# Softplus sums and dt times x on GpSimd, and an autoregressive part read from four token phases, in a hybrid scan, attention and spectral-convolution kernel

## Chip, cores and metric

The kernel runs on one core of one Trainium2 chip. The metric is the device time of one execution in microseconds; the median of several executions is quoted. Before the change it took 7304.48 us (three runs, 7297.25 to 7325.35).

## The reference, cut to what matters

Four images of 48 x 48 tokens with 128 channels pass two layers. The first has a selective scan in four directions:

```python
dt = softplus(dts + dt_proj_b)                      # 256 channels, 2304 tokens, 4 directions
def step(h, inp):
    dA = exp(dt_l[..., None] * A)                   # 16 states per channel
    h = h * dA + (dt_l * u_l)[..., None] * B_l
    y = einsum('bkdn,bkn->bkd', h, C_l)
# ... norm, gate, projection; then attention over 2304 tokens; then
def _stu(u, ...):                                   # four sequence lengths T, T/2, T/4, T/8
    return _compute_spectral(...) + _compute_ar_u(Mu, u)    # 16 long convolutions; 3 taps: u(t), u(t-1), u(t-2)
```

The change touches softplus and `dt * u` in the scan, and `_compute_ar_u`.

## The kernel before

Names used below: rep is a half's dt and dt * x, repeated for the states; bc is a row of B or C, spread over the partitions; xd holds a chunk's projected x; M are the mixture's matrices, G the convolution's output weights made from them, tt its filter tiles; a burst is a row of transfers or of GpSimd operations issued together.

An image's scan is one stage of 24 chunks (4 directions x 6 chunks of 384 tokens). A chunk has 8 units j = 0 to 7: two halves h of the channels times four groups q of the states. Stage 0 runs beside the "mixture" that prepares the convolution's weights; stages 1 to 3 run beside the convolution of the image before; the last convolution runs alone. Here is the preparation of a chunk, a generator that the scan loop advances by one `yield` twice a unit:

```python
ps = mm_tile(f"dt{name}_{h}")                                  # for each half h
nc.tensor.matmul(ps[:, :CS], dtw[:, k, h * P:(h + 1) * P], xd[:R + 1], start=True, stop=True)
nc.scalar.activation(re[:, h, 1], ps[:, :CS], AF.Abs)
nc.scalar.activation(re[:, h, 0], ps[:, :CS], AF.Relu)
# ... both halves: e = exp(-|.|), u = e + 1, l = ln(u), u = u - 1; then for each half h:
ps = mm_tile(f"sp{name}_{h}")
for i, (w, t) in enumerate(((ident, e[:, h]), (nident, u[:, h]), (ident, l[:, h]), (ident, re[:, h, 0]))):
    nc.tensor.matmul(ps[:, :CS], w, t, start=(i == 0), stop=(i == 3))       # softplus as a sum in PSUM
nc.scalar.copy(re[:, h, 0], ps[:, :CS])
nc.vector.tensor_tensor(re[:, h, 1]..., ps[:, :CS]..., x, ALU.mult)         # dt * x
# ... store re to DRAM; one unit after the other:  load(0), then load(1):
rep = pool.rep.tile([P, 2, G4, CS], F32, tag="rep", ...)
for c in range(C4):
    nc.sync.dma_start(rep[c * DL:(c + 1) * DL], d[h])                       # 4 x 384 KB
```

A unit multiplies by B (GpSimd for three of the eight units, `POOLED`, VectorE for the others), scans four times on VectorE, and multiplies by C on GpSimd; TensorE then sums the states into y. An engine takes its instructions in the program's order, here that of the scan loop:

```python
POOLED = ((0, 3), (1, 1), (1, 3))
enter(s)                              # B product: GpSimd for a pooled unit s+2, VectorE for unit s+1
units[s].scan(0, ...)                 # exp on ScalarE into PSUM, scan on VectorE
units[s - 1].times_c()                # GpSimd, 128x1536
units[s].scan(1, ...)
prepare(s)                            # one step of the next chunk's preparation (two chunks' for j = 4 and 5)
more((s + 0.5) / len(units))          # mixture or convolution, in equal shares of TensorE columns
units[s].scan(2, ...); units[s].scan(3, ...)
units[s - 2].sum_c(...)               # y on TensorE, waits for times_c of s-2
more(...); prepare(s)
```

The mixture loads its matrices M right ahead of use, and the convolution's short loads G and tt come from the same queue, SP's, as the rep loads:

```python
for k in range(KF):                   # mixture
    M = [pool.two.tile([P, NF, C], F32, tag=f"M{j}", ...) for j in range(2)]
    for t, src in zip(M, ("M_phi_plus", "M_phi_minus")):
        nc.sync.dma_start(t, a[src][:, k].rearrange("i d e -> d i e"))
# autoregressive part: tap j reads tokens (4 m + phase - j), a step of 4 tokens
src = now["x"][:, 2 - j:2 - j + 4 * w].rearrange("p (m r f) -> p f r m", f=2, r=2)
nc.tensor.matmul(p[:, :, :, :v], now["mu"][:, x, j, :], src[:, :, :, :v], ...)
```

Of the kernel before, what the change touches and what calls it, by code (L numbers as in the profile page):

```python
# [15 lines left out]
P = 128  # L16
B, H, W, C = 4, 48, 48, 128
L = H * W
# [34 lines left out]
def hybrid_kernel(ctx: ExitStack, tc: tile.TileContext, a: dict, out: bass.AP):  # L53
# [75 lines left out]

    zs = res.tile([NH, P, L], F32, name="zd")  # L130
    td = res.tile([L, C], F32, name="td")
    ud = res.tile([P, 2 + L], F32, name="ud")
    gd = res.tile([KF, P, 2, 2 * NF - 2, C], F32, name="gd")
    mud = res.tile([P, 2 * NF - 2, 3, C], F32, name="mud")
    fd = res.tile([KF, 3, 2, LF + P], F32, name="fd")
# [150 lines left out]
    class Chunk:  # L286
# [16 lines left out]
        def prep(self, pool):  # L303




            k, name, xc = self.k, self.name, xcs[self.b]
            yield
            xd = self.xd = pool.xd.tile([64, CS], F32, tag="xd", name=f"xd{name}")  # L310
            bcd = self.bcd = dram.tile([32, CS], F32, tag="bcd", name=f"bcd{name}")
            ps = mm_tile(f"xp{name}")
            for h in range(NH):
                nc.tensor.matmul(ps[:64, :CS], xw[:, h, k, :], in_order(xc[h], k, self.lo, CS),  # L314
                                 start=(h == 0), stop=(h == NH - 1))
            yield 2 * CS
            nc.scalar.activation(xd, ps[:64, :CS], AF.Identity, bias=onerow)
            yield

            u, l = [pool.one.tile([P, NH, CS], F32, tag=f"tmp{v}", name=f"{v}{name}") for v in "ul"]  # L320
            re = pool.one.tile([P, NH, 2, CS], F32, tag="re", name=f"re{name}")
            for h in range(NH):
                ps = mm_tile(f"dt{name}_{h}")
                nc.tensor.matmul(ps[:, :CS], dtw[:, k, h * P:(h + 1) * P], xd[:R + 1], start=True, stop=True)  # L324
                yield CS
                nc.scalar.activation(re[:, h, 1], ps[:, :CS], AF.Abs)
                nc.scalar.activation(re[:, h, 0], ps[:, :CS], AF.Relu)
                if h == 0:
                    nc.sync.dma_start(bcd, xd[32:64])
                yield  # L330
            e = re[:, :, 1]
            yield 0
            nc.scalar.activation(e, e, AF.Exp, scale=-1.0)
            nc.scalar.activation(u, e, AF.Identity, bias=1.0)
            yield
            yield 0
            nc.scalar.activation(l, u, AF.Ln)
            nc.scalar.activation(u, u, AF.Identity, bias=mone)
            d = dram.tile([NH, DL, 2, G4, CS], F32, tag="dtdu", name=f"dtdud{name}")

            def store(h):
                for g in range(G4):
                    nc.sync.dma_start(d[h, :, :, g], re[g * DL:(g + 1) * DL, h])

            def load(h):
                rep = pool.rep.tile([P, 2, G4, CS], F32, tag="rep", name=f"rep{name}_{h}")
                for c in range(C4):
                    nc.sync.dma_start(rep[c * DL:(c + 1) * DL], d[h])
                self.rep.append(rep)

            yield
            for h in range(NH):
                ps = mm_tile(f"sp{name}_{h}")
                for i, (w, t) in enumerate(((ident, e[:, h]), (nident, u[:, h]), (ident, l[:, h]), (ident, re[:, h, 0]))):
                    nc.tensor.matmul(ps[:, :CS], w, t, start=(i == 0), stop=(i == 3))  # L355
                yield 4 * CS

                nc.scalar.copy(re[:, h, 0], ps[:, :CS])
                x = in_order(xc[h], k, self.lo, CS)
                w = x.shape[2]  # L360
                nc.vector.tensor_tensor(re[:, h, 1].rearrange("p (r w) -> p r w", w=w),  # L361
                                        ps[:, :CS].rearrange("p (r w) -> p r w", w=w), x, ALU.mult)
                if h == 1:
                    store(0)
                yield
            yield 0
            store(1)
            load(0)
            yield
            yield 0  # L370
            load(1)
            yield

        def fetch(self, i, pool):
# [62 lines left out]
    EARLY = 4  # L437
    FETCHED = sorted({q for h, q in POOLED} | set(range(Q4, 2 * Q4)))

    CHUNK_COLS = (len(quads) - len(POOLED)) * CS + len(quads) * CS + 12 * CS  # L440

    def begin_scans(b, pool):

# [12 lines left out]
    def scans(b, chunks, preps, front, back, work, work_cols):  # L456

        units = [Unit(ch, h, q) for ch in chunks for h, q in quads]
        total = len(chunks) * CHUNK_COLS + work_cols
        done = [0]  # L460

        def more(share):

            while done[0] < share * total:
                cols = next(work, None)
                if cols is None:
                    break
                done[0] += cols

        def enter(s):  # L470

            if s + 2 < len(units) and units[s + 2].pool:
                units[s + 2].enter(back.s)
            if 0 <= s + 1 < len(units) and not units[s + 1].pool:
                units[s + 1].enter(back.s)

        def spread(s):
            if s < len(units) and not units[s].pool:
                units[s].spread(back.psB)
                done[0] += CS  # L480

        def prepare(s):

            ci, j = divmod(s, len(quads))
            for c in [ci + 1] * (j <= TURN + 1) + [ci + 2] * (j >= TURN):
                if c < len(chunks):
                    done[0] += next(preps[c], None) or 0

        def refill(s, i):

            if 0 <= s < len(units) and s // len(quads) + 1 < len(chunks):
                u, nxt = units[s], chunks[s // len(quads) + 1]
                if u.h == NH - 1:
                    nxt.fetch(i + u.q, front)

        pending = []
        spread(0)
        enter(-2)
        enter(-1)
        spread(1)  # L500
        for s in range(len(units) + 2):
            real = s < len(units)
            if pending and real:
                pending.pop().add_y()
            enter(s)
            if real:
                units[s].scan(0, back.psa)
            if 1 <= s <= len(units):
                units[s - 1].times_c()
            if real:  # L510
                units[s].scan(1, back.psa)
            prepare(s)
            more((s + 0.5) / len(units))
            spread(s + 2)
            if real:
                units[s].scan(2, back.psa)
                units[s].scan(3, back.psa)
            if pending:
                pending.pop().add_y()
            refill(s - 3, Q4)  # L520
            if s + 1 < len(units) and units[s + 1].pool:
                refill(s + 1, 0)
            if s >= 2:
                units[s - 2].sum_c(back.psy)
                done[0] += CS
                if units[s - 2].q == Q4 - 1:
                    pending.append(units[s - 2])
            more((s + 1) / len(units))
            prepare(s)
        for u in pending:  # L530
            u.add_y()
        assert next(work, None) is None
# [225 lines left out]
    def begin_stu(b, T, pool, ps):  # L758
# [7 lines left out]
        whole = L // 512  # L766
        nc.sync.dma_start(t[:, :whole], td[:512 * whole].rearrange("(J p j) c -> p J j c", p=P, j=4))
        nc.sync.dma_start(t[:KP[-1], whole], td[512 * whole:].rearrange("(p j) c -> p j c", j=4))
        uT = pool.one.tile([P, 2 + L], F32, tag="uT", name=f"uT{b}")
        nc.vector.memset(uT[:, 0:2], 0.0)  # L770
        yield
        for J in range(NM):
            k = KP[J]
# [3 lines left out]
            p = ps.pss.tile([P, 512], F32, tag="s", name=f"utr{b}_{J}")  # L777
            for j in range(4):
                nc.tensor.transpose(p[:, j * k:(j + 1) * k], u[:k, J, j], ident[:k, :k])
            nc.scalar.copy(uT[:, 2 + 512 * J:2 + 512 * J + 4 * k].rearrange("c (p j) -> c j p", j=4),  # L780
                           p[:, :4 * k].rearrange("c (j p) -> c j p", j=4))
        nc.sync.dma_start(ud, uT)

    STU_COLS = sum(KF * 12 * sum(hi - max(lo, J * P) for J in range((hi + P - 1) // P))
# [2 lines left out]
    def stu(b, pool, ps):  # L787
# [86 lines left out]
        def begin(n):  # L874
            (lo, hi, place, extra), k = items[n]
            m = 2 if extra else 1
            now["x"] = pool.one.tile([P, 2 + 512], F32, tag="ux", name=f"ux{b}_{n}")
            nc.sync.dma_start(now["x"][:, :2 + 4 * (hi - lo)], ud[:, 4 * lo:4 * hi + 2])
            now["mu"] = pool.one.tile([P, 2, 3, C], F32, tag="mue", name=f"mue{b}_{n}")
            nc.sync.dma_start(now["mu"][:, :m], mud[:, place:place + m])  # L880
            now["T", n] = pool.two.tile([P, 4, C], F32, tag="res", name=f"res{b}_{n}")
# [6 lines left out]
        def ar(n):  # L888
# [4 lines left out]
            now["p"] = p = p[:, :4 * w].rearrange("p (f r m) -> p f r m", f=2, r=2)  # L893
            for i, (v, x) in enumerate(parts(w, extra)):
                for j in range(3):
                    src = now["x"][:, 2 - j:2 - j + 4 * w].rearrange("p (m r f) -> p f r m", f=2, r=2)
                    nc.tensor.matmul(p[:, :, :, :v], now["mu"][:, x, j, :], src[:, :, :, :v],  # L897
                                     start=(i == 0 and j == 0), stop=False)
            yield 3 * 4 * (w + extra)
# [70 lines left out]
    activate(0)  # L970
    turn.close()
    begin0.close()
    front = Stage(tc, "f0", "left", one=(1, SB), xd=(3, SB), rep=(3, SB))
    begun = last(begin_scans(0, front))
    start_y(0)
    once = Stage(tc, "once", "right", one=(1, SB))
# [2 lines left out]
    for b in range(B):  # L979
# [24 lines left out]
        turn.close()  # L1004
        if b + 1 < B:
            activate(b + 1)
            front = Stage(tc, f"f{b + 1}", "left", one=(1, SB), xd=(3, SB), rep=(3, SB))
            pieces = begin_scans(b + 1, front)
        else:
            pieces = iter(())  # L1010
# [67 lines left out]
```

## Time and profile before

Engine names: PE is TensorE's matmuls, DVE VectorE, ACT ScalarE, POOL GpSimd, SP the queue from which nearly all transfers are issued. A stage runs from its first scan to its last.

| stretch of the profiled run | us |
|---|---|
| stage 0 (with the mixture) | 1055.5 |
| stages 1, 2, 3 (with a convolution) | 1351.6, 1345.2, 1336.5 |
| last convolution | 1026 |
| between them (attention, norms, start) | 1183 |

Stages 1 to 3 in the view of busy time by window; the columns are window, length, busy time (and number) of PE, PEld, DVE, ACT, POOL, then granted TensorE clock, DMA share, GB/s:

```profile
1555.10:2906.70 1351.60, 1287.80 (x5760) 733.50 (x5760) 1076.34 (x1305) 618.19 (x1177) 930.32 (x423) 0.97 0.67 174
3249.30:4594.50 1345.20, 1280.45 (x5760) 728.70 (x5760) 1076.45 (x1305) 618.14 (x1177) 930.35 (x423) 0.98 0.67 174
4935.10:6271.60 1336.50, 1272.04 (x5764) 723.37 (x5766) 1075.94 (x1305) 618.26 (x1177) 930.23 (x423) 0.99 0.68 176
```

The page's slices of the granted clock, its chain of waits by engine, and the median landing time of a rep load (last figure) in its list of transfers:

```profile
PEclk6777777979999998979999999879999999889999
...
PE 67%; DVE 18%; DMA 6%; ACT 3%; POOL 2%; issue 2%; SPq 2%; DVEq 0%; POOLq 0%; ACTq 0%
...
rep<-dtdud SPq DMA_DIRECT2D x768, 384.0 KB, 7.9
```

And TensorE's own waits over the whole run (total us, times, longest):

```profile
PE y L424 <- POOL s L416: 153.1, 66, 5.6
...
PE G L750 <- DMA M<-in_M_phi_plus: 103.4, 16, 7.3
...
PE pr L907 <- DMA G<-gd: 38.0, 13, 7.3
PE cv L851 <- DMA tt<-fd: 33.6, 13, 8.4
```

### The profile page before, as it was taken

How to read it: one execution, taken by the hardware profiler on the slowest of the kernel's cores; microseconds unless marked ns; L12 is line 12 of the kernel's file. 1: busy time of each engine (PE TensorE's matmuls, PEld its weight loads, DVE VectorE, ACT ScalarE, POOL GpSimd, SP SyncE). 2: the span in 40 equal slices, each digit the busy share in tenths (PEclk: the TensorE clock that was granted, in tenths of full speed). 3: DMA queues.
4: the chain of work that ended last, by engine and by line, in shares of the span. 5: the costliest groups of instructions: out<-in, count | busy, mean ns of one | idle time of the engine just before them, and what ended most of it. 6: DMA issues, size and time to landing. Idle time of an engine off the chain costs nothing.

```text
span 7297.7 us, 79952 instructions
## 1 busy us (share of the span) xinstructions
PE 6349.7 (87%) x26904; PEld 3623.1 (50%) x26904; DVE 4800.5 (66%) x5958; ACT 3042.6 (42%) x5979; POOL 3802.0 (52%) x1751
## 2 busy tenths in 40 slices
PE   3777776858999999858999999858999999779999
PEld 1332333424555566524555556523455556537778
DVE  5898887347888886347888886427888887412111
ACT  2666664434445543434444543334444544331000
POOL 1888886036777775016677776105677776200000
PEclk6777777979999998979999999879999999889999
DMA  3555553046676775025776767115666777215545
GB/s 76 138 141 138 135 138 90 18 114 151 171 180 178 192 190 163 27 74 142 169 185 169 193 181 204 38 52 140 165 179 172 192 180 210 67 41 136 153 138 175
DMA packets 630989, 1021.01 MB, mean 140 GB/s; under 512 B 87178, under 2 KB 488202, under 8 KB 605331
## 3 DMA queue, kind: packets, MB, share of 16 engines
q1 hardware_dynamic: 627600, 1015.13, 53.4%
q8 instruction: 214, 3.51, 0.2%
q14 instruction: 197, 1.61, 0.1%
q10 hardware_dynamic: 2978, 0.77, 0.1%
HBM read 897.72 MB, written 117.85 MB: 139 GB/s over the span
## 4 chain that ended last, share of the span: by engine, by line
PE 67%; DVE 18%; DMA 6%; ACT 3%; POOL 2%; issue 2%; SPq 2%; DVEq 0%; POOLq 0%; ACTq 0%
PE cv L851 28%; DVE s L407 9%; PE pr L907 8%; PE y L424 6%; PE sp L355 5%; PE B L391 4%; PE s L643 4%; DVE s L399 4%; PE o L634 3%; PE xp L314 2%; PE pr L897 2%; DMA G<-gd 2%; PE dt L324 2%; DVE xc L246 1%; DMA tt<-fd 1%
## 5 line engine op out<-in xcount | busy, mean ns | idle before, releaser
L416 POOL TENSOR_TENSOR s<-s,bc 128x1536 f32<-128x1536 f32 x768 | 2647.5, 3448 | 267.2 <-DVE s L407 173.7
L407 DVE TENSOR_TENSOR_SCAN s<-dA,carry,s 128x384 f32<-128x384 f32 x2560 | 2441.0, 1001 | 252.9 <-ACT dA L404 251.4
L404 ACT ACTIVATE dA<-rep,A 128x384 f32<-128x384 f32 x3072 | 1752.9, 584 | 964.7 <-DVE s L407 950.6
L851 PE MATMUL cv<-tt,u 128*128 128x256 f32 (+4 forms) x7680 | 1683.3, 358 | 54.3 <-DVE U L871 38.0
L851 PEld LDWEIGHTS cv<-tt,u 128*128 128x128 f32 (+1 forms) x7680 | 1271.0, 190 | 668.3 <-issue 343.7
L871 DVE TENSOR_TENSOR U<-cv,Q 128x256 f32<-128x256 f32 (+1 forms) x1280 | 494.6, 392 | 1057.2 <-PE cv L851 1054.7
L399 POOL TENSOR_TENSOR s<-rep,bc 128x1536 f32<-128x1536 f32 x288 | 993.9, 3451 | 31.5 <-DMA ud<-uT 22.8
L851 PE MATMUL cv<-tt,us 128*128 128x256 f32 (+4 forms) x3840 | 873.2, 363 | 79.4 <-DVE U L871 39.4
L399 DVE TENSOR_TENSOR s<-rep,B 128x1536 f32<-128x1536 f32 x480 | 834.6, 1739 | 71.3 <-PE B L391 60.0
L424 PE MATMUL y<-s,csum 128*32 128x384 f32 x6144 | 717.1, 541 | 170.8 <-POOL s L416 153.1
L860 ACT COPY Q<-cv 128x256 f32<-128x256 f32 (+3 forms) x640 | 224.6, 352 | 1393.1 <-PE cv L851 1262.3
L851 PEld LDWEIGHTS cv<-tt,us 128*128 128x128 f32 (+1 forms) x3840 | 638.5, 192 | 322.2 <-issue 95.4
L907 PE MATMUL pr<-U,G 128*128 128x512 f32 (+4 forms) x2048 | 716.5, 481 | 46.3 <-DMA G<-gd 38.0
L415 POOL COPY carry<-s 128x4 f32<-128x4 f32 x640 | 121.3, 190 | 1107.2 <-DVE s L407 1038.8
L391 PE MATMUL B<-xd,spread 32*128 32x384 f32 x960 | 474.3, 576 | 57.5 <-DVE s L399 57.4
L407 DVE TENSOR_TENSOR_SCAN s<-dA,s 128x384 f32<-128x384 f32 x512 | 457.0, 939 | 38.7 <-ACT dA L404 37.7
L156 POOL TENSOR_TENSOR ln_vu<-ln_vu,mhalf 128x4 f32<-128x4 f32 (+1 forms) x20 | 20.1, 1007 | 854.3 <-DVE ln_vu L155 854.3
L907 PEld LDWEIGHTS pr<-U,G 128*128 128x128 f32 x2048 | 339.5, 194 | 249.2 <-issue 145.8
L424 PEld LDWEIGHTS y<-s,csum 128*32 128x32 f32 x6144 | 125.7, 111 | 608.0 <-issue 294.8
L644 ACT ACTIVATE e<-s,shift 128x512 f32<-128x512 f32 (+1 forms) x360 | 232.0, 644 | 311.9 <-PE s L643 309.1
L643 PE MATMUL s<-xnT 128*128 128x512 f32 (+1 forms) x720 | 342.4, 560 | 1.6 <-ACT e L644 1.6
L355 PE MATMUL sp<-re,ident 128*128 128x384 f32 x768 | 324.0, 504 | 17.8 <-DVE re L361 16.1
(158 smaller groups left out, 4865.2 us busy)
## 6 DMA issues: line engine op xcount, KB each, us to landing
rep<-dtdud SPq DMA_DIRECT2D x768, 384.0 KB, 7.9
tt<-fd SPq DMA_DIRECT2D x192, 577.0 KB, 4.1
bc<-bcd SPq DMA_DIRECT2D x2304, 48.0 KB, 3.7
tt<-fd SPq DMA_DIRECT2D x192, 513.0 KB, 4.3
tt<-fd SPq DMA_DIRECT2D x192, 385.0 KB, 3.9
dtdud<-re SPq DMA_DIRECT2D x768, 96.0 KB, 2.2
G<-gd SPq DMA_DIRECT2D x192, 256.0 KB, 4.7
tt<-fd SPq DMA_DIRECT2D x64, 514.0 KB, 5.2
```

The source lines that it names most:

```text
L355: nc.tensor.matmul(ps[:, :CS], w, t, start=(i == 0), stop=(i == 3))
L391: nc.tensor.matmul(self.bt[:, :CS], spread[32:64, self.q].rearrange("p c j -> p (c j)"), self.ch.xd[32:64], start=True, stop=True)
L399: eng.tensor_tensor(s, self.ch.rep[self.h][:, 1], bt.unsqueeze(1).to_broadcast([P, G4, CS]), ALU.mult)
L404: nc.scalar.activation(dA[:, :CS], ch.rep[self.h][:, 0, g], AF.Exp, scale=A[:, ch.k, self.h * G4 + g, self.q:self.q + 1])
L407: nc.vector.tensor_tensor_scan(s, dA[:, CS - 1::-1] if ch.rev else dA[:, :CS], s, 0.0 if ch.first else carry[:, self.h, self.q, g:g + 1], ...
L416: nc.gpsimd.tensor_tensor(self.s, self.s, ch.bc[Q4 + self.q].unsqueeze(1).to_broadcast([P, G4, CS]), ALU.mult)
L424: nc.tensor.matmul(ch.y[g * DL:(g + 1) * DL, :CS], csum, self.s[:, g], start=(self.q == 0), stop=(self.q == Q4 - 1))
L643: nc.tensor.matmul(p[:, :w], xnT[:, i * P:(i + 1) * P], xnT[:, lo:lo + w], start=True, stop=True)
L644: nc.scalar.activation(nxt[:, lo:lo + w], p[:, :w], AF.Exp, bias=shift, accum_out=sm[:, i, q:q + 1])
L851: nc.tensor.matmul(p2[:, :, at - first:], x, t[:kp, :, hi - 1 - at + J * P:end if end >= 0 else None:-1], start=(J == 0), stop=(J == nb - 1))
L871: nc.vector.tensor_tensor(dst, src, q, ALU.add)
L907: nc.tensor.matmul(p[:, :, :v], Gs[n][:, q, x, :], U[n][:, 4 * q:4 * q + 4, :v], start=False, stop=(k == KF - 1 and q == 1 and v == w))
```

## The change

Its intent is to relieve TensorE, the bound of stages 1 to 3, of eight products a chunk, and VectorE and ScalarE of a product and a copy, by giving sums and products to GpSimd; and to read the autoregressive taps in runs instead of every fourth token. Buffers for xd go from three to two, which pays for the larger tile.

```diff
             nc.scalar.activation(l, u, AF.Ln)
             nc.scalar.activation(u, u, AF.Identity, bias=mone)
+            nc.gpsimd.tensor_tensor(u, e, u, ALU.subtract)
+            nc.gpsimd.tensor_tensor(r, r, u, ALU.add)
+            yield
+            ...                                         # three more yields
+            nc.gpsimd.tensor_tensor(r, r, l, ALU.add)
+            for h in range(NH):
+                x = in_order(xc[h], k, self.lo, CS)
+                ...
+                nc.gpsimd.tensor_tensor(dx, dt, x, ALU.mult)
+            yield
+            yield 0
+            for h in range(NH):                         # stores, both halves
+                for g in range(G4):
+                    nc.sync.dma_start(d[h, :, :, g], re[g * DL:(g + 1) * DL, h])
+            yield
+            yield 0
+            for h in range(NH):                         # loads, both halves in one step
+                rep = pool.rep.tile(...)
+                for c in range(C4):
+                    nc.sync.dma_start(rep[c * DL:(c + 1) * DL], d[h])
-            ...                                         # ident/nident matmuls, copy, DVE product, store(0); store(1), load(0); load(1)
-            for c in [ci + 1] * (j <= TURN + 1) + [ci + 2] * (j >= TURN):
+            for c in [ci + 1] * (j <= TURN) + [ci + 2] * (j >= TURN):
-            now["x"] = pool.one.tile([P, 2 + 512], F32, tag="ux", ...)
-            nc.sync.dma_start(now["x"][:, :2 + 4 * (hi - lo)], ud[:, 4 * lo:4 * hi + 2])
+            now["x"] = pool.one.tile([P, 6, P], F32, tag="ux", ...)
+            nc.sync.dma_start(now["x"][:, 2:, :hi - lo], ud[:, :, 1 + lo:1 + hi])
+            nc.sync.dma_start(now["x"][:, :2, :hi - lo], ud[:, 2:, lo:hi])
-                    src = now["x"][:, 2 - j:2 - j + 4 * w].rearrange("p (m r f) -> p f r m", f=2, r=2)
+                    src = now["x"][:, 2 - j:6 - j].rearrange("p (r f) m -> p f r m", f=2)
-    front = Stage(tc, "f0", "left", one=(1, SB), xd=(3, SB), rep=(3, SB))
+    front = Stage(tc, "f0", "left", one=(1, SB), xd=(2, SB), rep=(3, SB))
```

The cut leaves out that the columns counted for a chunk's preparation (CHUNK_COLS) fall from 12 to 4 times 384, which shifts where the mixture's and the convolution's pieces come in a chunk.

More of the change, by code (lines that the diff above doesn't have):

```diff
@@ L131, in hybrid_kernel @@
     td = res.tile([L, C], F32, name="td")
-    ud = res.tile([P, 2 + L], F32, name="ud")
+    ud = res.tile([P, 4, 1 + LF], F32, name="ud")
     gd = res.tile([KF, P, 2, 2 * NF - 2, C], F32, name="gd")
@@ L329, in prep @@
                     nc.sync.dma_start(bcd, xd[32:64])
-                yield
-            e = re[:, :, 1]
-            yield 0
+                    yield
+            r, e = re[:, :, 0], re[:, :, 1]
             nc.scalar.activation(e, e, AF.Exp, scale=-1.0)
@@ L338, in prep @@
             nc.scalar.activation(u, u, AF.Identity, bias=mone)
+            nc.gpsimd.tensor_tensor(u, e, u, ALU.subtract)
[7 more added lines that the diff above has]
+                x = in_order(xc[h], k, self.lo, CS)
+                dt, dx = (re[:, h, i].rearrange("p (r w) -> p r w", w=x.shape[2]) for i in range(2))
+                nc.gpsimd.tensor_tensor(dx, dt, x, ALU.mult)
+            yield
+            yield 0
             d = dram.tile([NH, DL, 2, G4, CS], F32, tag="dtdu", name=f"dtdud{name}")
-            def store(h):
+            for h in range(NH):
                 for g in range(G4):
                     nc.sync.dma_start(d[h, :, :, g], re[g * DL:(g + 1) * DL, h])
-            def load(h):
+            yield
+            yield 0
+            for h in range(NH):
                 rep = pool.rep.tile([P, 2, G4, CS], F32, tag="rep", name=f"rep{name}_{h}")
@@ L349, in load @@
                 self.rep.append(rep)
-            yield
-            for h in range(NH):
-                ps = mm_tile(f"sp{name}_{h}")
-                for i, (w, t) in enumerate(((ident, e[:, h]), (nident, u[:, h]), (ident, l[:, h]), (ident, re[:, h, 0]))):
-                    nc.tensor.matmul(ps[:, :CS], w, t, start=(i == 0), stop=(i == 3))
-                yield 4 * CS
-                nc.scalar.copy(re[:, h, 0], ps[:, :CS])
-                x = in_order(xc[h], k, self.lo, CS)
-                w = x.shape[2]
-                nc.vector.tensor_tensor(re[:, h, 1].rearrange("p (r w) -> p r w", w=w),
-                                        ps[:, :CS].rearrange("p (r w) -> p r w", w=w), x, ALU.mult)
-                if h == 1:
-                    store(0)
-                yield
-            yield 0
-            store(1)
-            load(0)
-            yield
-            yield 0
-            load(1)
             yield
@@ L438, in hybrid_kernel @@
     FETCHED = sorted({q for h, q in POOLED} | set(range(Q4, 2 * Q4)))
-    CHUNK_COLS = (len(quads) - len(POOLED)) * CS + len(quads) * CS + 12 * CS
+    CHUNK_COLS = (len(quads) - len(POOLED)) * CS + len(quads) * CS + 4 * CS
     def begin_scans(b, pool):
@@ L768, in begin_stu @@
         nc.sync.dma_start(t[:KP[-1], whole], td[512 * whole:].rearrange("(p j) c -> p j c", j=4))
-        uT = pool.one.tile([P, 2 + L], F32, tag="uT", name=f"uT{b}")
-        nc.vector.memset(uT[:, 0:2], 0.0)
+        uT = pool.one.tile([P, 4, 1 + LF], F32, tag="uT", name=f"uT{b}")
+        nc.vector.memset(uT[:, :, 0:1], 0.0)
         yield
@@ L779, in begin_stu @@
                 nc.tensor.transpose(p[:, j * k:(j + 1) * k], u[:k, J, j], ident[:k, :k])
-            nc.scalar.copy(uT[:, 2 + 512 * J:2 + 512 * J + 4 * k].rearrange("c (p j) -> c j p", j=4),
-                           p[:, :4 * k].rearrange("c (j p) -> c j p", j=4))
+            nc.scalar.copy(uT[:, :, 1 + J * P:1 + J * P + k], p[:, :4 * k].rearrange("c (j p) -> c j p", j=4))
         nc.sync.dma_start(ud, uT)
@@ L876, in begin @@
             m = 2 if extra else 1
-            now["x"] = pool.one.tile([P, 2 + 512], F32, tag="ux", name=f"ux{b}_{n}")
-            nc.sync.dma_start(now["x"][:, :2 + 4 * (hi - lo)], ud[:, 4 * lo:4 * hi + 2])
+            now["x"] = pool.one.tile([P, 6, P], F32, tag="ux", name=f"ux{b}_{n}")
+            nc.sync.dma_start(now["x"][:, 2:, :hi - lo], ud[:, :, 1 + lo:1 + hi])
+            nc.sync.dma_start(now["x"][:, :2, :hi - lo], ud[:, 2:, lo:hi])
             now["mu"] = pool.one.tile([P, 2, 3, C], F32, tag="mue", name=f"mue{b}_{n}")
@@ L1006, in hybrid_kernel @@
             activate(b + 1)
-            front = Stage(tc, f"f{b + 1}", "left", one=(1, SB), xd=(3, SB), rep=(3, SB))
+            front = Stage(tc, f"f{b + 1}", "left", one=(1, SB), xd=(2, SB), rep=(3, SB))
             pieces = begin_scans(b + 1, front)
```

## The prediction

> **What bounds the kernel now.** I read the page's busy shares and slices first, then the chain of waits, then the busy time of each engine by stage, then the groups of instructions. The whole page names TensorE as busiest, but its slices and chain show stages with different limits:
>
> ```profile
> PE 6349.7 (87%) x26904; PEld 3623.1 (50%) x26904; DVE 4800.5 (66%) x5958; ACT 3042.6 (42%) x5979; POOL 3802.0 (52%) x1751
> ...
> PE   3777776858999999858999999858999999779999
> ...
> DVE  5898887347888886347888886427888887412111
> ...
> POOL 1888886036777775016677776105677776200000
> ...
> PE cv L851 28%; DVE s L407 9%; PE pr L907 8%; PE y L424 6%; PE sp L355 5%; PE B L391 4%; PE s L643 4%; DVE s L399 4%; PE o L634 3%; PE xp L314 2%; PE pr L897 2%; DMA G<-gd 2%; PE dt L324 2%; DVE xc L246 1%; DMA tt<-fd 1%
> ```
>
> Four scan stages (one per image, 24 chunks each) show as the runs of high POOL digits. In the first, PE digits are 7 while DVE and POOL stand at 8. In the other three, which carry the spectral convolution of the image before, PE is at 9. The chain's "sp L355 5%" is the work that the change removes (4.9% in the unrounded chain, 358 us).
>
> I took each stage from its first scan to its last and asked for the engines' busy time there. The columns are window, length, then busy time of PE, PEld, DVE, ACT, POOL, clock, DMA share, GB/s. The first line is stage 0, the next three are stage 1 cut at chunks 7 and 20.
>
> ```profile
> 160.20:1215.70 1055.50, 795.36 (x3068) 325.26 (x3066) 949.46 (x980) 642.19 (x1196) 923.91 (x423) 0.75 0.56 135
> ```
> ```profile
> 1555.10:1975.30 420.20, 380.43 (x1504) 193.77 (x1504) 325.25 (x412) 188.11 (x364) 269.96 (x125) 0.96 0.65 157
> 1975.30:2652.80 677.50, 668.80 (x2915) 378.08 (x2914) 575.15 (x670) 337.92 (x631) 508.74 (x233) 0.99 0.70 181
> 2652.80:2906.70 253.90, 238.57 (x1345) 161.65 (x1344) 175.93 (x224) 92.16 (x183) 151.61 (x67) 0.92 0.64 181
> ```
>
> Stage 0 takes 44.0 us a chunk, with DVE busy 90% and POOL 88%: VectorE sets the pace and GpSimd has only 5.5 us a chunk to spare. Stage 1's 13 middle chunks take 52.1 us each and PE is busy for 98.7% of them: they are bound by TensorE. Its first 7 chunks (60.0 us) and last 4 (63.5 us) leave PE 6 to 10% idle, behind transfers and VectorE. Stages 2 and 3 take 1345 and 1337 us against 1352 and look alike. After the last scan only the convolution runs, on PE.
>
> The groups that the change touches, or that price it:
>
> ```profile
> L416 POOL TENSOR_TENSOR s<-s,bc 128x1536 f32<-128x1536 f32 x768 | 2647.5, 3448 | 267.2 <-DVE s L407 173.7 <-DMA bc<-bcd 16.7 <-PE cv L851 13.9
> L399 POOL TENSOR_TENSOR s<-rep,bc 128x1536 f32<-128x1536 f32 x288 | 993.9, 3451 | 31.5 <-DMA ud<-uT 22.8 <-DMA mud<-mum 8.7
> ...
> L361 DVE TENSOR_TENSOR re<-sp,xc 128x384 f32<-128x384 f32 x192 | 130.2, 678 | 119.5 <-ACT re L358 118.3
> L415 POOL COPY carry<-s 128x4 f32<-128x4 f32 x640 | 121.3, 190 | 1107.2 <-DVE s L407 1038.8 <-DMA bc<-bcd 28.8 <-DMA dtdud<-re 14.8
> ```
> ```profile
> L907 PE MATMUL pr<-U,G 128*128 128x512 f32 x1024 | 535.3, 611 | 0.0
> L897 PE MATMUL pr<-ux,mue 128*128 128x512 f32 x96 | 89.6, 1082 | 5.4 <-DMA mue<-mud 5.4
> ```
>
> The last two rows are the same shape, 128x512: the projection reads its moving operand in runs, the autoregressive part reads every fourth token, and a record takes 1082 ns instead of 611.
>
> **What the Trainium skill says.** "GPSIMD Engine Reference", section 3.1, gives about 2.6 cycles an element for a two-input operation and 4497 ns for 2048; the trace's 3448 ns for 1536 (2.2 ns an element) agrees. Its section 7 says that reads with a step over 8 bytes take about 2.9 cycles instead of 1.9; no GpSimd instruction of the trace before shows such a read, so I use the extra cycle as an estimate. "SBUF — State Buffer", section "Who interferes with whom", says that a DVE instruction with at most one SBUF input, outside the 2-port modes, doesn't contend with GpSimd. The scans and multiplications here have an operand in PSUM; the trace agrees, GpSimd's 768 products staying within 3418 to 3535 ns beside a DVE that is 90% busy. The same page's section "Door 1" speaks of 16-byte lines in which neighbouring fp32 reads are cheap; the 1082 against 611 ns at a 16-byte step agrees.
>
> **The change part by part.**
>
> *Removed from TensorE: the softplus sums.* Eight fp32 products of 384 columns a chunk. In a middle chunk of stage 1 their union is 5.5 us (16 records of 486 ns, overlapped). 23 chunks of a stage prepare a successor, so at most 23 x 5.5 = 127 us a stage, and 380 us in the three TensorE-bound stages, which fits the chain's 358. In stage 0 they are off the bound.
>
> *Removed elsewhere.* 192 ScalarE copies (92 us) and 192 VectorE products (130 us, 1.36 us a chunk), and the chain dt, sp, copy, product between four engines. VectorE's relief counts in stage 0 only if GpSimd doesn't take over.
>
> *Added to GpSimd.* Three sums of 768 elements and two products of 384 a chunk. With 0.2 us fixed (the 4-element copy takes 0.19) and (3.40 - 0.2)/1536 = 2.08 ns an element (3.40 us is the start-to-start spacing in the timeline): 1.8 us a sum and 1.0 us a product, 7.4 us a chunk. For the odd directions x is read with a 192-byte step; the skill's extra cycle makes a product 1.3 us and the chunk 8.0. Mean 7.7 us, 730 us over 96 chunks less the unprepared ones. GpSimd's busy time goes from 3802 to about 4540 us, and a chunk needs 923.9/24 + 0.5 for the gaps after the small copies + 7.7 = 46.7 us of it. I allow 1.3 us of idle for its waits on ScalarE: a floor of **48 us a chunk**.
>
> *Stage 0.* 48 is above 44.0, so GpSimd becomes the bound: 23 x 48 + 37 for the last chunk, which prepares nothing, is 1141, or **+85 us**.
>
> *Stages 1 to 3.* Each chunk becomes the larger of its present time less 5.5 and 48. By stretch: 7 x 5.5 + 13 x (52.1 - 48) + 3 x 5.5 = 108; chunk by chunk, since the middle ones vary from 49 to 57 us, 101. Two engines close to their limit wait for each other at times; I take back 17. So **-84 a stage, -252 in all**: GpSimd's floor keeps a third of what TensorE gives up.
>
> *Autoregressive part.* 192 records busy for 121.7 us. At the projection's time for each shape they would take about 75: -47, or -12 a convolution. In full in the last stage, about two thirds in the others, where some fall into the GpSimd-bound middle: **-36 us**. One more transfer at each block's start is issued blocks ahead of nothing but the first, about +1 us each; the PSUM copies without a strided write return about as much.
>
> *Head of each image.* For image 0 the sums run from 91.4 to 102.3 us on the chain; GpSimd needs 7.4 us, so -3. For the others the path runs through transfers: 0 to +3. Together about 0.
>
> *Buffers.* Two xd instead of three: the next chunk's xd is written after the last B product that reads the old one, by program order, so no new wait.
>
> Sum: 7304 + 85 - 252 - 36 = **7101 us**.
>
> **The rivals.** *GpSimd caps everything.* Its work is uneven: units 0 to 3 of a chunk carry the two bursts and two pooled products, about 29 us against some 22 of the other engines, units 4 to 7 only 18. If the y sums on TensorE wait in the burst and GpSimd starves after it, a chunk takes 51 us, not 48: +153 in stage 0, -67 in the others, about 7215. For it: TensorE already waits 153 us for these products. Against: the six s buffers let VectorE run some two units ahead. *TensorE stays the only bound.* If the floor never shows in stages 1 to 3, they give -127 each, and with VectorE-paced stage 0 little lost: about 6950. Against: 46.7 us is nearly the middle chunk's 52.1 - 5.5. *The transfers become the wait.* The stores now follow GpSimd, which runs behind VectorE, and both rep loads (1.5 MB each, some 8 us) go together; if they land after VectorE needs them, each chunk loses 1 to 3 us, up to +200. I count three units, 18 us, between load and need, so it mostly hides. *Clock.* PE is granted 0.75 in stage 0, where it idles, and 0.97 to 0.99 when full; less work in stages 1 to 3 could lower it and give back some of the gain.
>
> **Range and chances.** The midpoint 7101 is 2.8% faster. The main uncertainties are GpSimd's floor (each us of it moves about 23 + 3 x 11 = 55 us) and the coupling, in each case to the slow side more than the fast. I set 6990 to 7220. Faster by over 2% needs under 7158, a floor under about 49 us: 0.74. Within 2%: 0.24. Slower: 0.02.
>
> **What would show it.** GpSimd busy near 4540 us, 768-element sums near 1.8 us, the odd directions' products longer; stage 0 longer at about 1140 us with GpSimd over 95% busy and the chain moved onto it; stages 1 to 3 near 1265 us, with middle chunks at 48 to 50; autoregressive 512-column records near 611 ns. I am wrong if the sums take much more than 1.8 us, if TensorE's wait for s or a wait for rep grows to several us a chunk, or if stage 0 hardly moves.

## The result and the profile after

The changed kernel took 7563.31 us (median of four, 7552.61 to 7571.41) against 7301.56 us of the kernel before in the same rounds: slower, by a ratio of 1.0351 with an interval of 1.0323 to 1.0379. A ratio is the mean time of one kernel's runs over the mean of the other's of the same rounds, so not quite the ratio of the medians.

The page after, shares, slices and chain of waits:

```profile
PE 6012.5 (80%) x25368; PEld 3413.4 (45%) x25368; DVE 4668.1 (62%) x5766; ACT 2971.6 (39%) x5787; POOL 4501.6 (60%) x2231
...
PE   3555555676898998785898999795898998889999
...
POOL 2888888505788987404788887505788897500000
PEclk6666666787899998897899998897898998889999
...
PE 35%; DMA 23%; issue 12%; DVE 12%; POOL 11%; SPq 4%; ACT 2%; POOLq 0%; DVEq 0%; ACTq 0%
...
rep<-dtdud SPq DMA_DIRECT2D x768, 384.0 KB, 11.1
```

TensorE's share of the chain falls from 67% to 35% and the transfers' share goes from 6% to 23%; the clock is a step lower in many slices of the four stages; a rep load lands in 11.1 us instead of 7.9. By window, the four stages and the last convolution:

```profile
162.20:1409.50 1247.30, 714.17 (x2695) 267.15 (x2695) 923.69 (x934) 619.48 (x1156) 1086.16 (x536) 0.63 0.48 114
1752.60:3126.20 1373.60, 1209.05 (x5400) 682.51 (x5400) 1040.71 (x1259) 603.96 (x1129) 1094.78 (x536) 0.92 0.68 170
3466.20:4839.50 1373.30, 1214.33 (x5400) 683.51 (x5400) 1041.24 (x1259) 604.02 (x1129) 1094.94 (x536) 0.92 0.68 170
5179.60:6542.80 1363.20, 1204.61 (x5400) 680.89 (x5400) 1041.19 (x1259) 604.11 (x1129) 1094.96 (x536) 0.92 0.69 171
6542.80:7554.00 1011.20, 933.27 (x4120) 694.67 (x4120) 187.79 (x451) 150.50 (x386) 16.01 (x10) 0.95 0.39 120
```

Stage 0 is 192 us longer, stages 1 to 3 are 22, 28 and 27 us longer, the last convolution is 15 us shorter and the rest adds 3: together the 257 us between the two profiled spans. The groups that the prediction priced (after their engine, operation and shape: busy us, mean ns of one):

```profile
L338 POOL TENSOR_TENSOR u<-re,u 128x768 f32<-128x768 f32 x96 | 174.2, 1815 | 559.2 <-ACT u L337 556.9 <-DMA bc<-bcd 2.0
L349 POOL TENSOR_TENSOR re<-re,xc 128x384 f32<-128x384 f32 x192 | 206.1, 1094 | 7.5
L889 PE MATMUL pr<-ux,mue 128*128 128x512 f32 x96 | 51.9, 684 | 8.3 <-DMA mue<-mud 8.3
```

These sizes were right. What went wrong is in TensorE's waits:

```profile
PE y L415 <- POOL s L407: 347.7, 115, 7.6
PE G L741 <- DMA M<-in_M_phi_plus: 215.8, 15, 23.1
PE pr L899 <- DMA G<-gd: 132.9, 23, 11.1
PE cv L841 <- DMA tt<-fd: 122.4, 36, 9.5
```

Against the same rows of before, the wait for M has doubled and those for G and tt are three and a half times as long. In stage 0 the chunks, measured from the first scan of one to the first of the next, go 43.6, 47.7, 64.8, 47.7, 47.7, 64.7 us and so on, every third one long. One of the long ones in the timeline, first TensorE, then SP's queue (start, length, and in brackets the idle time before it and its releaser):

```profile
913.17 2.93 PE L741 MATMUL G<-M,W 128*128 128x128 f32 x12
938.60 1.62 PE L741 MATMUL G<-M,W 128*128 128x384 f32 x2 [22.50 <-DMA M<-in_M_phi_plus]
940.15 1.64 PE L382 MATMUL B<-xd,spread 32*128 32x384 f32 x2
```
```profile
919.79 3.73 SPq L361 DMA_DIRECT2D rep<-dtdud  x8
924.24 0.34 SPq L747 DMA_DIRECT2D gd<-Gm  x1
926.12 0.40 SPq L724 DMA_DIRECT2D M<-in_M_phi_plus  x1
```

The eight rep loads (3 MB) leave SP from 919.8 us; M is issued at 926.1, behind them, and TensorE, in order, has it only at 938.6: 12.5 us from issue to use, where a load of M took 3.4 us in the median before. The other 10.0 us of TensorE's idle time passed before M was issued: SP stood 10.5 us at the stores until GpSimd's first dt * x was done (914.6), then issued eight stores and eight rep loads. So M came late for two reasons, its place behind stores and loads in the program, and the burst in front of it. Behind TensorE's 22.5 us of idle stands the B product that VectorE's next unit needs, so scans and GpSimd stop too. The Trainium skill, "DMA: Bandwidth & Descriptors", section "Two DMAs through the same engine are not ordered", says that within one queue of one DMA engine descriptors start in order; a small load behind 3 MB then waits for them, and the trace agrees: by its landing records the last rep load landed at 937.0 and M at 938.5.

### The profile page after: what moved, and what is told of

The parts are those of the page before. It is cut to its first block, busy times and chain, and to the rows that moved or that the text cites. A ratio compares the mean times of both kernels' runs of the same rounds, so it can differ in the third digit from the quotient of the medians. Undisturbed runs are those within 1.5% of the kernel's fastest.

```text
span 7554.2 us, 77318 instructions
## 1 busy us (share of the span) xinstructions
PE 6012.5 (80%) x25368; PEld 3413.4 (45%) x25368; DVE 4668.1 (62%) x5766; ACT 2971.6 (39%) x5787; POOL 4501.6 (60%) x2231
## 4 chain that ended last, share of the span: by engine, by line
PE 35%; DMA 23%; issue 12%; DVE 12%; POOL 11%; SPq 4%; ACT 2%; POOLq 0%; DVEq 0%; ACTq 0%
PE cv L841 18%; DMA rep<-dtdud 8%; DVE s L398 7%; DMA tt<-fd 6%; POOL s L407 5%; PE pr L899 5%; DMA G<-gd 3%; PE y L415 3%; POOL s L390 3%; DMA bc<-bcd 2%; PE B L382 2%; DVE s L390 2%; SPq L355 2%; POOL re L345 1%; SPq L369 1%
## 5 line engine op out<-in xcount | busy, mean ns | idle before, releaser
L841 PE MATMUL cv<-tt,u 128*128 128x256 f32 (+4 forms) x7680 | 1726.9, 367 | 143.7 <-DVE U L861 71.7
L841 PEld LDWEIGHTS cv<-tt,u 128*128 128x128 f32 (+1 forms) x7680 | 1307.7, 196 | 743.4 <-issue 375.7
L415 PE MATMUL y<-s,csum 128*32 128x384 f32 x6144 | 784.6, 588 | 362.8 <-POOL s L407 347.7
L899 PE MATMUL pr<-U,G 128*128 128x512 f32 (+4 forms) x2048 | 766.5, 507 | 136.1 <-DMA G<-gd 132.9
L382 PE MATMUL B<-xd,spread 32*128 32x384 f32 x960 | 501.0, 605 | 115.2 <-DVE s L390 114.8
L338 POOL TENSOR_TENSOR u<-re,u 128x768 f32<-128x768 f32 x96 | 174.2, 1815 | 559.2 <-ACT u L337 556.9
L741 PE MATMUL G<-M,W 128*128 128x128 f32 (+2 forms) x768 | 247.9, 477 | 216.9 <-DMA M<-in_M_phi_plus 215.8
## 6 DMA issues: line engine op xcount, KB each, us to landing
rep<-dtdud SPq DMA_DIRECT2D x768, 384.0 KB, 11.1
```

The lines of the kernel that those rows point to most:

```text
L382: nc.tensor.matmul(self.bt[:, :CS], spread[32:64, self.q].rearrange("p c j -> p (c j)"), self.ch.xd[32:64], start=True, stop=True)
L415: nc.tensor.matmul(ch.y[g * DL:(g + 1) * DL, :CS], csum, self.s[:, g], start=(self.q == 0), stop=(self.q == Q4 - 1))
L741: nc.tensor.matmul(p[:, :n] if j else p[:, NF - 1 - i], W[:, q if t else 0, i], M[t][:, i].unsqueeze(1).to_broadcast([P, n, C]) if j else ...
L841: nc.tensor.matmul(p2[:, :, at - first:], x, t[:kp, :, hi - 1 - at + J * P:end if end >= 0 else None:-1], start=(J == 0), stop=(J == nb - 1))
L899: nc.tensor.matmul(p[:, :, :v], Gs[n][:, q, x, :], U[n][:, 4 * q:4 * q + 4, :v], start=False, stop=(k == KF - 1 and q == 1 and v == w))
```

## The experiments

**Theory.** The rep loads in one burst delay other loads of the same queue; TensorE stops at those, and its stops lower its clock. **Rivals:** GpSimd's own load and its coupling to TensorE; the stores that wait for GpSimd in SP's queue; three rep buffers for two tiles a chunk.

The stage lengths of the profiled runs, in us, with the runs' median times:

| run | stage 0 | stages 1, 2, 3 | median | ratio to before (interval) |
|---|---|---|---|---|
| before | 1056 | 1352, 1345, 1337 | 7301.56 | |
| after | 1247 | 1374, 1373, 1363 | 7563.31 | 1.0351 (1.0323 to 1.0379) |
| e1_split | 1198 | 1318, 1317, 1320 | 7357.32 | 1.007 (1.005 to 1.009) |
| e2_mix | 1125 | 1371, 1371, 1367 | 7459.17 | 1.0218 (1.0201 to 1.0236) |
| e3_ar | 1054 | 1339, 1345, 1325 | 7251.03 | 0.993 (0.9913 to 0.9947) |
| e4_before_mix | 1001 | 1350, 1336, 1345 | 7246.95 | 0.9918 (0.9903 to 0.9933) |
| e5_split_mix | 1126 | 1321, 1320, 1320 | 7287.95 | 0.9976 (0.9959 to 0.9993) |
| e6_relief | 1063 | 1296, 1284, 1292 | 7114.97 | 0.9739 (0.9724 to 0.9753) |
| e7_dead | 1121 | 1400, 1404, 1389 | 7501.32 | 1.0266 (1.0249 to 1.0283) |
| e8_before_ar_mix | 1001 | 1340, 1339, 1329 | 7198.15 | 0.9856 (0.9839 to 0.9873) |
| e9_relief_more | 1024 | 1330, 1336, 1329 | 7209.98 | 0.9865 (0.9848 to 0.9882) |
| e10_early | 1063 | 1285, 1288, 1286 | 7102.31 | 0.9716 (0.9701 to 0.973) |
| e11_g3 | 1060 | 1271, 1273, 1285 | 7065.52 | 0.9664 (0.9643 to 0.9684) |
| e12_early_g3 | 1066 | 1272, 1276, 1285 | 7094.88 | 0.9712 (0.9699 to 0.9725) |

All gave correct outputs. The stages are those of the one profiled run of each kernel.

### e1_split: one rep load at a time

```diff
                 self.rep.append(rep)
-            yield
+                yield
+                if h == 0:
+                    yield 0
-            for c in [ci + 1] * (j <= TURN) + ...
+            for c in [ci + 1] * (j <= TURN + 1) + ...
```

> The kernel after, with the two rep loads of a chunk issued one unit apart, as in the kernel before, and not together. Theory (transfers: 3 MB in one burst hold up the mixture's and the convolution's own loads, and TensorE stops at them): the mixture's load stands behind one rep load in place of two, some 8 us less, so the 64.8 us chunks of stage 0 come down to about 57 and the stage from 1247 to about 1190 us; stages 1 to 3 from 1370 to about 1340; total about 7410 us. Rival A (GpSimd's floor and its coupling with TensorE cause the loss in stages 1 to 3): stages 1 to 3 stay within 10 us of 1370, total about 7500. Rival B (the stores' wait for GpSimd in the SP queue is what holds the loads up): stage 0 stays within 20 us of 1247.

The kernel is 206 us faster than the kernel after, by nothing but issuing the second of two transfers a unit later. Its stage 1 by window, and TensorE's waits over the run:

```profile
1700.60:3018.70 1318.10, 1192.14 (x5400) 676.90 (x5400) 1040.81 (x1259) 603.21 (x1129) 1095.16 (x536) 0.94 0.72 177
```
```profile
PE cv L843 <- DMA tt<-fd: 63.5, 27, 8.3
...
PE pr L901 <- DMA G<-gd: 55.1, 17, 5.9
```

The long chunks of stage 0 come down from 64.8 to 57.5 us, stages 1 to 3 by 43 to 56 us, the clock goes from 0.92 to 0.94. TensorE's waits for G and tt fall from 132.9 and 122.4 us to 55.1 and 63.5. The gain in stages 1 to 3 is larger than expected (about 1340). Rivals A and B, as stated, are out: GpSimd's work and the stores are the same in both kernels. As parts of the loss they are not: GpSimd's load is priced below, and the long chunks of stage 0 are still 10 us over the others, with M behind the stores and one rep load.

### e2_mix: the mixture's loads one k ahead

```diff
-        for k in range(KF):
-            M = [...]; nc.sync.dma_start(...)            # loads of k
+        ahead = fetch(0)
+        for k in range(KF):
+            M, ahead = ahead, fetch(k + 1) if k + 1 < KF else None
```

> The kernel after, with the mixture's loads issued one k ahead of their use. Theory: the seven 17 us excesses of stage 0 are TensorE's wait for these loads, and vanish: every chunk 47 to 49 us, stage 0 from 1247 to about 1135 us; stages 1 to 3 as in the kernel after (1374, 1373, 1363 within 10); total about 7450 us. Rival (every third chunk is long because three rep buffers serve two tiles a chunk, whatever the mixture does): stage 0 keeps its 64.8 us chunks, total about 7560.

```profile
162.70:1287.90 1125.20, 724.97 (x2692) 272.42 (x2692) 921.85 (x934) 619.89 (x1156) 1085.90 (x536) 0.65 0.52 126
```

Stage 0 loses 122 us and chunks 1 to 21 (counted from 0) take 46.5 to 48.1 us each, with GpSimd busy for 96.5% of the stage (1085.90 of 1125.20): the floor that the prediction put at 48. The stages with the convolution do not move. The rival of the three rep buffers is out: they are still three.

### e3_ar: the autoregressive part alone

The kernel before with the second half of the change's diff (from `now["x"]` on) and two xd buffers.

> The kernel before with the four token phases of the autoregressive part and the two xd buffers alone; the softplus sums stay on TensorE and VectorE. Prediction's step: 512-column records near 680 ns in place of 1082, some 12 us a convolution: last stage 1026 to about 1013, total about 7304 - 45 = 7259 us. Rival (the second transfer at each block start costs what the matmuls save): within 10 us of the kernel before.

It is 57 us faster than the kernel before; the last convolution takes 1009 us instead of 1026. So this part of the change is a gain by itself, and the loss lies in the other. The two xd buffers were not tried apart from it. In the profiled runs the gain is 47 us, 18 of it in the last convolution.

### e4_before_mix: the mixture's loads ahead, in the kernel before

The edit of e2 on the kernel before.

> The kernel before, with the mixture's loads one k ahead. Theory: they were exposed before the change too (103 us of TensorE's wait in stage 0), and VectorE then paces the stage: 1055 down to about 990 us, the 47 us chunks to 41; total about 7240 us. Rival (VectorE and GpSimd absorb that wait, as they are the busier engines): stage 0 stays above 1040, total within 15 us of the kernel before.

Stage 0 falls by 54 us (65 expected), so TensorE's wait for M was on the path before as well. VectorE is then busy 95% of it (948.49 of 1001.40 us).

### e5_split_mix: both mends

The edits of e1 and e2 on the kernel after.

> The kernel after with both mends of the transfers: rep loads one unit apart and the mixture's loads one k ahead. Theory (the two are separate victims of one queue): the gains add in stages where each acts: stage 0 as in e2_mix (1125), stages 1 to 3 as in e1_split (1318 each): total about 7285 us. Rival (a stage made shorter meets the next limit at once): above 7330.

The two add, to 3 us of the expectation. The kernel after with its transfers mended is level with the kernel before. What remains is not the transfers alone: stages 1 to 3 are 1320 us, where the prediction had near 1265.

### e6_relief: one pooled product back to VectorE

```diff
-    POOLED = ((0, 3), (1, 1), (1, 3))
+    POOLED = ((0, 3), (1, 3))
```

> e5_split_mix with one of the three pooled products of a chunk given back to VectorE (128x1536, 3.4 us less for GpSimd, 1.7 us more for VectorE, 0.6 us more for TensorE). Theory (GpSimd's 47 us a chunk is the floor of stage 0 and one cause of TensorE's idle gaps in the others): stage 0 falls by 3.4 x 23 = 78 us to about 1050, stages 1 to 3 from 1318 to about 1290, total about 7120 us. Rival (stages 1 to 3 are bound by TensorE, by its lower granted clock and by transfers): stage 0 falls, stages 1 to 3 rise by some 15 us each for the added matmul; total about 7250 us.

```profile
159.80:1222.40 1062.60, 787.69 (x2748) 287.03 (x2748) 962.89 (x958) 620.19 (x1156) 1008.23 (x512) 0.65 0.54 129
1561.10:2857.20 1296.10, 1205.45 (x5448) 677.79 (x5448) 1079.24 (x1283) 604.62 (x1129) 1014.80 (x512) 0.95 0.72 177
```

The expected 7120 us came out at 7115, and this kernel beats both. Stages 1 to 3 got 25 to 35 us shorter although TensorE was given a matmul more: that speaks for GpSimd's load as their brake. It is not alone in the edit: without that product on GpSimd its row of B isn't loaded, so SP issues 1920 bc loads of 48 KB instead of 2304. How much of the gain is theirs was not tried.

### e7_dead: the products back on TensorE as dead work

```diff
+            for h in range(NH):
+                ps = mm_tile(f"dead{name}_{h}")
+                for i in range(4):
+                    nc.tensor.matmul(ps[:, :CS], nident if i == 1 else ident, l[:, h], start=(i == 0), stop=(i == 3))
+                yield 4 * CS
-    CHUNK_COLS = ... + 4 * CS
+    CHUNK_COLS = ... + 12 * CS
```

> e5_split_mix with the eight 384-column products a chunk put back on TensorE as dead work (their result is not used; the output stays correct). It measures what taking them off TensorE is worth by itself. The prediction's model (stages 1 to 3 gain the larger of TensorE's relief and GpSimd's floor): about +101 us a stage, +300 us in all. Theory (TensorE now waits for GpSimd and transfers, and its clock falls when it waits, so that the relief is worth less): granted clock back from 0.94 to 0.96 or more, +50 to +70 us a stage, total +150 to +210 us over e5. Rival (the relief is worth nothing): within 60 us of e5.

```profile
1628.00:2949.10 1321.10, 1191.98 (x5400) 677.04 (x5400) 1041.40 (x1259) 603.11 (x1129) 1095.35 (x536) 0.94 0.72 177
```
```profile
1622.70:3022.70 1400.00, 1303.82 (x5764) 743.50 (x5765) 1048.43 (x1259) 598.18 (x1129) 1095.02 (x536) 0.95 0.67 168
```

The first line is stage 1 of e5, the second of e7: 112 us of TensorE work cost 79 us in stage 1, and 78 us on average of the three; over the run 213 us. That lies above the expected 50 to 70 a stage and 150 to 210 in all, and below the 101 of the prediction's model. The clock rose only to 0.95 in two stages and 0.96 in one, less than expected. This run splits the mended change in two. Taking the products off TensorE is worth 78 us a stage. Giving the work to GpSimd costs 61 us a stage (1398 on average here against 1336 in e3, which has the same TensorE work and the old engines), net of what VectorE and ScalarE save. The split takes the dead products, which nothing waits for, to stand for the old ones.

### e8_before_ar_mix: what needs no GpSimd

> The kernel before with the four token phases and with the mixture's loads one k ahead; the softplus sums stay on TensorE and VectorE. The gains of e3_ar (57 us) and e4_before_mix (61 us) are in different stages and should add: about 7190 us.

The gains of e3 and e4, 57 and 61 us, nearly add: 104 us. It is the fair opponent for the versions with the moved sums: e6 and e11 beat it by 83 and 133 us in the medians (e11 in another session; by the ratios to the kernel before, 1.9%). But e5, which differs from e8 only by the moved sums and the places of the stores and loads that go with them, is 90 us slower: 124 us longer in stage 0 and 16 shorter on average in stages 1 to 3. So moving the sums is a loss even with the transfers mended, until a product is given back. The third G buffer was not tried in e8.

### e9_relief_more: a second product back

```diff
-    POOLED = ((0, 3), (1, 3))
+    POOLED = ((1, 3),)
```

> e6_relief with a second pooled product given back to VectorE, so that one of three stays on GpSimd. Theory (in e6 GpSimd at 43.5 us a chunk still paces stage 0, VectorE stands at 40.1): stage 0 becomes VectorE's, 41.8 + 2 us of idle, so about 1050 (1063 in e6); stages 1 to 3 lose the added matmul, 0.6 x 24 = 15 us each, or gain as much if GpSimd still holds TensorE up: total within 45 us of 7115, more likely above. Rival (GpSimd is still the main brake of stages 1 to 3): total below 7060.

This missed: 95 us more than e6, where up to 45 were expected. Stage 0 gained 38 us, now with VectorE busy 97% (997.37 of 1024.10). Stages 1 to 3 lost 34 to 52 us each. In stage 1, TensorE's busy time rose by 30 us, twice the 15 that the added matmuls take, and its waits for VectorE's U from 46 to 60 us. GpSimd was relieved and the stage was longer, so one product less is the balance, not two. That doubling was not looked into. The loads are those of e6 here, so of the two only GpSimd's work changed.

### e10_early, e11_g3, e12_early_g3

e10 moves GpSimd's last sum and products one unit ahead of where they stood (two `yield`s go from before them to after them). e11 gives G three buffers and fetches it one item further ahead:

```diff
-                Gs[n] = pool.two.tile([P, 2, 2, C], F32, tag="G", ...)
+                Gs[n] = pool.three.tile([P, 2, 2, C], F32, tag="G", ...)
-                        fetch_G(n)
+                        fetch_G(n + 1)
```

> e6_relief with GpSimd's last sum and the two products issued one unit earlier, so that the stores in the SP queue find their operands ready. Theory Rival B (the stores' wait for GpSimd, 604 us in e6's SP queue, holds other loads up): that wait falls below 350 us, TensorE's waits for G and tt fall, stages 1 to 3 from 1291 to about 1270: total about 7050 us. Other theory (that wait was there before the change as well, 701 us, and the loads have slack for it): total within 30 us of 7115.

> e6_relief with three G buffers and G fetched one item further ahead. Theory (short items at a stage's start meet the rep loads, G's lead of one item is then too short, and each such gap also costs clock): TensorE's wait for G falls from some 15 us a stage to near 0, stages 1 to 3 each 15 to 25 us shorter: total about 7055 us. Rival (tt, which has the same queue, is then the wait): within 20 us of 7115.

> e6_relief with both e10_early and e11_g3. The two act on the same waits (TensorE's for G), so they should not add: between 7035 and 7065 us. If they add in full: 7053. If the earlier sums crowd GpSimd's burst: above 7080.

In e10 the stores' wait for GpSimd in SP's queue fell from 604 to 350 us, TensorE's waits for G and tt fell from 37.5 and 52.2 to 8.9 and 21.1 us, but its wait for GpSimd's s rose from 169 to 236 us, which a denser burst would explain; that was argued, not tried. At 7102 us it lies in the range of the other theory (within 30 of 7115), and the ratio's interval overlaps that of e6. In e11 the wait for G no longer appears in the list, stages 1 to 3 are 7 to 25 us shorter than in e6, and at 7065.52 us it is the fastest kernel. One thing doesn't fit the simple tale: rep loads land in 10.9 us in e6 and e11, nearly as late as in the kernel after, and yet the waits for G and tt are shorter. Why the two loads meet again there was not followed up. e12 missed its range; at 7095 us it lies where the expectation put a crowded burst of GpSimd (above 7080), and TensorE's wait for s is 232 us, against 185 in e11. Its profiled stages are within 6 us of those of e11, but the profiled run was its fastest (7083), so why its median is 29 us longer stays open.

## Why the prediction was wrong, step by step

**GpSimd's sizes: right.** 1815 ns for a sum (1.8 us predicted), 999 ns for a product of the even directions (1.0) and 1190 for the odd ones (1.3); busy time 4501.6 us (4540).

**GpSimd's floor of 48 us in stage 0: right.** 46.5 to 48.1 us in the chunks of e2, and 1125 us for the stage once M is loaded ahead (1141 predicted).

**The step that failed: "I count three units, 18 us, between load and need, so it mostly hides."** It asked only whether the rep loads come in time for their own users. They did: no engine that reads rep has a wait for it in its list, beyond 19 us of ScalarE in pieces of at most 1.5. The burst hurt others: M, G and tt, issued later in the same queue and needed sooner. It cost 206 us (after against e1): 49 in stage 0 and 51 on average in each of stages 1 to 3. The prediction had named the burst, with up to +200 us, but for rep loads that come late to VectorE, and dismissed it; that its figure is near 206 is luck.

**A term that the sum lacked: the wait for M in stage 0.** The prediction read the stage as paced by VectorE, then by GpSimd. With the rep loads spaced it still took 1198 us, and M loaded ahead took off 73 more (1125, e5 against e1). Before the change M was exposed too, by 54 us (e4). So the stage's 192 us in place of the predicted 85 are 70 of the floor (1125 against 1055), 73 of M and 49 of the burst.

**"Each chunk becomes the larger of its present time less 5.5 and 48", "-84 a stage": too large, even with the transfers mended.** e5 stands 24 us a stage below the kernel before, some 8 of which are the autoregressive part by e3. In place of TensorE's full 127 us the relief was worth 78 (e7), and in place of 43 us for floor and coupling (the two engines' waits for each other) GpSimd's load cost 61 (e7 against e3).

**"Clock", named as a rival without a price: it did fall.** From 0.97 to 0.99 it went to 0.92 in stages 1 to 3. The clock records in the trace have TensorE at half its clock for 36 to 78 us in each of stages 1 to 3 before, 210 to 217 us after and 159 to 163 us in e1. Its busy time in a stage fell by 71 us on average (1280 to 1209), where the removed work, 127 + 12, would take it down by 139. The Trainium skill, "TensorE: Matmul & The Clock Gate", section "HAM oscillation — how this bites in real kernels", has idle gaps of more than about 3.4 us put the array back to half its clock. The trace agrees in part: such gaps number 2 or 3 in each of these stages before (13 to 17 us together) and 12 or 13 after (74 to 78 us, the longest 11). But they aren't needed: in e10 TensorE never stood still for more than 3.1 us in these stages and had half its clock for 109 to 123 us in each. No run moved the clock by itself, so its share of the loss is argued, not shown.

**Autoregressive part: right in its direction, larger than predicted.** 684 ns in place of 1082 (611 predicted), 15 us in the last convolution (12 predicted), 57 us for the part with its buffers alone (36 predicted).

**The sum.** 7563 - 7101 = 462 us. 206 of it are the two rep loads in one step (after against e1), 69 the wait for M that stays when they are spaced (e1 against e5). The other 187 are the mended change's smaller gain, 7288 against 7101, mostly in stages 1 to 3. (One sum of the rivals doesn't come out: 7304 - 3 x 127 - 36 is 6887, not 6950, unless stage 0 is to lose some 60 us.)

## What to carry to other kernels

Ask of a moved or merged transfer not only whether its own reader can wait, but what stands behind it in its queue and how soon an in-order engine needs that; short loads needed soon belong ahead of bulk loads, or further ahead in time. An engine relieved of work that then waits more often may lose part of the relief to a lower clock (not shown here by itself), so a relief is priced by putting the work back as dead work in the new kernel. When work goes to a second engine that is itself near its limit, rebalance the old work as well: here the change by itself lost 3.5%; with its transfers spaced, M loaded ahead, one product given back and a third buffer it gained 3.4%, of which 1.4% come without the moved sums (e8).

## What the Trainium skill lacked or had wrong

- "GPSIMD Engine Reference", section 7: about one cycle an element more for reads with a large step. Measured on a 128x384 product with one of two inputs at a 192-byte step: 1190 against 999 ns, 0.6 cycles an element at the page's 1.2 GHz; the page does not say how the step counts in a two-input operation.
- "DMA: Bandwidth & Descriptors": the start order within a queue is there, but not what a bulk load does to a short one behind it. Here two 1.5 MB loads in one step instead of two spaced ones cost 206 us of 7563, and one 256 KB load was in use only 12.5 us after its issue, where the median landed in 3.4 before.
- "TensorE: Matmul & The Clock Gate": it ties the clock to how busy TensorE has been and tells of waits and short idle times, but has no case in which taking work off TensorE lowers the clock. Here eight fp32 products less a chunk went with a granted clock of 0.92 instead of 0.97 to 0.99, and 0.94 with the transfers mended; dead work of that size put back (e7) raised it to 0.95 and 0.96.
